# One more step of distance at four places of the second layer's interleaved chains, in a two-layer perceiver block on one core

## The chip, the core and the metric

The kernel runs on one core of one Trainium2 chip. The metric is the device time of one execution in microseconds (us), as the median of several runs. One execution was also recorded by the hardware profiler; times inside the kernel come from that record. The engines are TensorE (PE, with its weight loads shown as PEld), VectorE (DVE), ScalarE (ACT), GpSimd (POOL) and SyncE (SP, which issues most DMAs).

## The reference

Sixteen sequences of 64 tokens, 256 wide, pass through two layers. Each layer is cross-attention to a context of 1024 rows per sequence (16 heads of 16), then a self-attention, then a feed-forward part; before each part the rows are normalised, and the result is added to `x`.

```python
x = x + L0_xattn(layernorm(x), ctx_1024, ...)
x = x + L0_attn(layernorm(x), ...)
x = x + L0_ffn(layernorm(x), ...)       # top-2 of 8 experts
x = x + L1_xattn(layernorm(x), ctx_1024, bias, mask, ...)
x = x + L1_attn(layernorm(x), ...)      # rotary positions, softmax over 64
x = x + L1_ffn(layernorm(x), ...)       # silu(gate) * up, all operands quantised

# the second layer's feed-forward quantises x, h and the weights:
scale = max(abs(block of 16)) / 6
q = nearest of (0, .5, 1, 1.5, 2, 3, 4, 6) to abs(x / scale), with sign, times scale
```

All arithmetic is in 32-bit floats.

## The kernel before, in words

Only the second layer is touched. It starts in the profile at about 864 us and is one call of `cross_attention(1, ...)` that also carries the self-attention and the feed-forward part as side chains.

The 1024 rows of `x` are held as eight tiles `x[n]` of 128 rows, two sequences each. The cross-attention walks over 64 slots: 16 sequences, two halves of the heads (`dt`), two halves of the 1024 keys (`hf`). For each slot, PE makes four score products (`scores`, L567), sixteen transposes in four groups (`transpose_keys`, L597, four groups of four heads) and sixteen products with the values (`attend`, L611). DVE adds the mask to the scores and takes minima (L578), ACT takes the exponentials once both key halves are there (L589), and DVE and ACT copy the transposed weights out of PSUM (L226, L228). Key and value projections of sequences that were not made earlier stand in the slots too (`project`, L394 and L409); the first nine sequences have theirs loaded from DRAM, so from about 1130 us on each slot holds more PE work.

The side chains are Python generators. After each of the four groups of transposes of a slot, `advance()` lets every live chain go on to its next `yield`. A step is thus a quarter of a slot, and `bare(n)` is n steps in which the chain issues nothing. What a chain issues in a step stands on PE between two groups of transposes. Three kinds of chain are of interest:

- `outputs(b)` ends the attention of sequence b: ACT copies the sum `ot`, PE turns it (L633), DVE divides by the sums into `osb` (L636); after the second sequence of a pair, PE turns `osb` (L649), DVE adds a bias into `oT` (L653), and `project_rows` multiplies by the output weights (L322) and adds to `x[n]` (L324).
- `row_attention(n)` follows: normalisation on DVE (`layernorm_rows`, L258 to L275), turning (`transposed_rows`, L290 and L292), query and key products (L1373), rotation (L1393), value products (L1416), scores (L1428), softmax, the weights turned (L1452) and copied by ACT into `turned` (L228), their products with the values (L1468, L1479), the division (L1489, L1490) and the projection (L322).
- `feed_forward(n)` follows that: normalisation, `fp4` quantisation of the row (L1037 to L1053, ten DVE instructions in three steps), turning, gate and up products in two halves (`hidden`, L1520) with a silu on ACT (L1523), `fp4` of each half, `turn_hidden(0)` and `turn_hidden(3)` (L1530), and the down product (L1545).

A chain for tile n starts when its second sequence is done, every 32 steps (eight slots), and is longer than that, so the feed-forward part of tile n runs beside `outputs` and `row_attention` of tile n + 1. `queries(n)` is a further chain, not changed here. After the last slot, a loop advances the chains that are left two steps at a time, with nothing in between: there a bare step alone separates nothing.

PE's order is the program's (`tc.manual_schedule(engines={PE})`). The orders of DVE, ACT and POOL are made by the tile framework's scheduler when the program is built, from the program's order and its own estimates. All engines execute in order. PSUM has eight banks: one for the attention sums (`pso`), seven handed out in rotation to all other products (`bank()`, tiles `psw`): the eighth `bank()` after another waits until the tile of the first has been read.

Of the kernel before, what the change touches and what calls it, by code (L numbers as in the profile page):

```python
# [120 lines left out]
def kernel(ctx: ExitStack, tc: tile.TileContext, a: dict, out: bass.AP):  # L121
# [17 lines left out]
    def bank():  # L139
        return psum["w"].tile([P, 512], F32, name="psw")  # L140
# [18 lines left out]
    def colbias(name, dt):  # L159
        j = KC * COLB.index(name) + dt  # L160
        return colb[:, j : j + 1]
# [16 lines left out]
    def rowbias(name):  # L178
        j = ROWB.index(name)
        k = j - NB0 if j >= NB0 else j  # L180
        return rowb[j >= NB0][:, D * k : D * (k + 1)]
# [40 lines left out]
    def evacuate(dst, src, vector=None):  # L222

        turn[0] += 1
        if turn[0] % 2 if vector is None else vector:
            nc.vector.tensor_copy(dst, src)  # L226
        else:
            nc.scalar.copy(dst, src)  # L228
# [21 lines left out]
    def bare(n):  # L250

        for _ in range(n):
            yield
# [33 lines left out]
    def transposed_rows(pool, xn, name="xTr"):  # L287
        pt = bank()
        for c in range(KC):
            nc.tensor.transpose(pt[:, c * P : (c + 1) * P], xn[:, c * P : (c + 1) * P], ident)  # L290
        xT = pool.tile([P, KC, P], F32, name=name)
        nc.scalar.copy(xT, pt[:, : 2 * P].rearrange("p (c t) -> p c t", c=KC))  # L292
        return xT
# [24 lines left out]
    def project_rows(n, oT, w, bias=None):  # L318

        pm = bank()  # L320
        for c in range(KC):
            nc.tensor.matmul(pm[:, :D], oT[:, c, :], w[:, c, :], start=(c == 0), stop=(c == KC - 1))  # L322
        if bias is None:
            nc.vector.tensor_tensor(x[n], pm[:, :D], x[n], ALU.add)  # L324
            return
        t = small.tile([P, D], F32, name="prow")
        nc.vector.tensor_tensor(t, pm[:, :D], bias, ALU.add)
        nc.gpsimd.tensor_tensor(x[n], x[n], t, ALU.add)


    def cross_attention(layer, wq, wkv, wo, bq, bk, bv, bo, mask, keep, bias, after, ready, arrive, idle):
        side = "right" if layer else "left"
        with ExitStack() as st:
# [285 lines left out]
            def outputs(b):  # L619


                n, half = b // 2, b % 2
                ot = two.tile([P, KC, P], F32, name="ot")
                evacuate(ot, po.pop(b), False)
                yield
                yield
                rec = two.tile([P, NP], F32, name="rec")
                nc.vector.reciprocal(rec, sums[b])
                if half == 0:
                    osb[n] = two.tile([P, NP, 2, HD], F32, name="osb")  # L630
                pq = bank()
                for c in range(KC):
                    nc.tensor.transpose(pq[:, c * P : (c + 1) * P], ot[:, c, :], ident)  # L633
                pov = pq[:, :D].rearrange("p (r j d) -> p r j d", j=2, d=HD)
                for j in range(2):
                    nc.vector.tensor_tensor(  # L636
                        osb[n][half * SQ : (half + 1) * SQ, :, j, :],
                        pov[j * SQ : (j + 1) * SQ, :, j, :],
                        rec[j * SQ : (j + 1) * SQ, :].unsqueeze(2).to_broadcast([SQ, NP, HD]),
                        ALU.mult,  # L640
                    )
                if half == 0:
                    return
                yield
                yield
                pt = bank()
                rows = osb[n].rearrange("p r j d -> p (r j d)")
                for c in range(KC):
                    nc.tensor.transpose(pt[:, c * P : (c + 1) * P], rows[:, c * P : (c + 1) * P], ident)  # L649
                oT = two.tile([P, KC, P], F32, name="oT")  # L650
                for c in range(KC):

                    nc.vector.tensor_scalar(  # L653
                        oT[:, c, :], pt[:, c * P : (c + 1) * P], colbias(bv, c), None, ALU.add
                    )
                yield
                yield
                project_rows(n, oT, wo, None if layer else rowbias(bo))
# [361 lines left out]
    def fp4_tiles(pool, tag, most):  # L1020
        return (
            pool.tile([P, most], F32, name=f"t{tag}"),
            pool.tile([P, most], F32, name=f"m{tag}"),
            pool.tile([P, most // BLK], F32, name=f"scl{tag}"),
            pool.tile([P, most // BLK], F32, name=f"rsc{tag}"),
        )
# [323 lines left out]
    def last_layers(one):  # L1350
# [11 lines left out]
        def row_attention(n, two):  # L1362
# [2 lines left out]
            nc.gpsimd.tensor_tensor(x[n], x[n], rowbias("L1_attn_b_proj"), ALU.add)  # L1365
            yield from bare(4)
            xT = transposed_rows(two, xn)
            yield
            yield
            pm = bank()  # L1370
            for i, (w, dt) in enumerate((w, dt) for w in (wq, wk) for dt in range(KC)):
                for c in range(KC):
# [76 lines left out]
            for dt in range(KC):  # L1449
# [5 lines left out]
                        ident,  # L1455
                    )
                evacuate(eT[:, dt, :, :], pt.rearrange("p (g q) -> p g q", g=NG), False)
            yield
            yield


            po = [bank() for _ in range(2)]
# [38 lines left out]
        def feed_forward(n, two):  # L1501
            tok = slice(n * P, (n + 1) * P)
            alone = n == NT - 1
            xn = yield from layernorm_rows(two, n, "xnr", True)
            yield
            yield from fp4(fp4_tiles(one, "h", NI), xn, xn, P, D)
            yield from bare(2)
            xT = transposed_rows(two, xn)
            yield
            yield  # L1510
            h = one.tile([P, NI], F32, name="h")
            hT = one.tile([P, NCH, P], F32, name="hT")

            def hidden(cols):
                w = cols.stop - cols.start
                pg = bank()[:, :w]
                pu = bank()[:, :w]
                for ps, wt in ((pg, wgT), (pu, wuT)):
                    for c in range(KC):
                        nc.tensor.matmul(  # L1520
                            ps, xT[:, c, :], wt[:, c, cols], start=(c == 0), stop=(c == KC - 1)
                        )
                nc.scalar.activation(h[:, cols], pg, AF.Silu)  # L1523
                nc.vector.tensor_tensor(h[:, cols], pu, h[:, cols], ALU.mult)

            def turn_hidden(g):
                pt = bank()
                for j in range(3):
                    w = min(P, NI - (g + j) * P)
                    nc.tensor.transpose(  # L1530
                        pt[:w, j * P : (j + 1) * P], h[:, (g + j) * P : (g + j) * P + w], ident
                    )
                if g + 3 < NCH:
                    evacuate(hT[:, g : g + 3, :], pt[:, : 3 * P].rearrange("p (j t) -> p j t", j=3), False)
                else:
                    evacuate(hT[:, g : g + 2, :], pt[:, : 2 * P].rearrange("p (j t) -> p j t", j=2), False)
                    w = NI - (g + 2) * P
                    evacuate(hT[:w, g + 2, :], pt[:w, 2 * P : 3 * P], False)

            py = None  # L1540

            def down(g):
                for j in range(g, g + 3):
                    w = min(P, NI - j * P)
                    nc.tensor.matmul(py, hT[:w, j, :], wdT[:w, j, :], start=(j == 0), stop=(j == NCH - 1))  # L1545


            halves = [slice(0, 3 * P), slice(3 * P, NI)]
            if alone:

                hidden(halves[0])
                tiles = fp4_tiles(one, "h", NI)
                first = fp4(tiles, h[:, halves[0]], h[:, halves[0]], P, 3 * P)
                next(first)
                hidden(halves[1])
                for _ in first:
                    pass
                turn_hidden(0)
                py = bank()[:, :D]
                down(0)  # L1560
                for _ in fp4(tiles, h[:, halves[1]], h[:, halves[1]], P, NI - 3 * P, 3 * P):
                    pass
                turn_hidden(3)
                down(3)
            else:
                tiles = fp4_tiles(one, "h", NI)
                hidden(halves[0])
                yield
                yield from fp4(tiles, h[:, halves[0]], h[:, halves[0]], P, 3 * P)
                hidden(halves[1])  # L1570
                yield
                turn_hidden(0)
                yield
                yield from fp4(tiles, h[:, halves[1]], h[:, halves[1]], P, NI - 3 * P, 3 * P)
                yield from bare(2)
                turn_hidden(3)
                yield from bare(3)
                py = bank()[:, :D]
                down(0)
                down(3)  # L1580
            y = small.tile([P, D], F32, name="prow")
            nc.vector.tensor_tensor(y, py, x[n], ALU.add)
            nc.sync.dma_start(of[tok, :], y)
# [104 lines left out]
```

## Time and profile before

| | |
|---|---|
| device time, three runs | 1530.3, 1532.1, 1533.7 us (median 1532.1) |
| profiled execution: its own time, its span | 1533.16 us, 1531.1 us |
| mean granted PE clock | 0.949 of full speed |
| PE busy | 1393.2 us, 91% |
| DVE busy | 953.7 us, 62% |
| ACT busy | 759.2 us, 50% |
| POOL busy | 336.2 us, 22% |
| second layer: start, last slot, end | about 864, 1455 and 1528 us |

"Idle before" is the time that an engine stood still ahead of an instruction, and the releaser after the arrow is the instruction whose end let it go on. PE is the busy engine, and it executes in order, so a wait of PE in the slots delays everything behind it. The granted clock is the share of full clock that PE was given in a stretch; at 0.50 a product takes about twice as long.

### The profile page before, as it was taken

The page shows a single profiled execution, that of the slowest core. Times are in us where ns is not written, and L with a number is a line of the kernel's source. Part 1 is how long each engine was busy: PE and PEld are TensorE (multiplying, and loading weights), DVE is VectorE, ACT ScalarE, POOL GpSimd, SP SyncE. Part 2 cuts the span into 40 slices and gives each one's busy share as a digit, 9 for nine tenths or more (in the row PEclk, how much of TensorE's full clock was granted, in tenths as well). Part 3 has the DMA queues.
Part 4 walks back from the last instruction along what each step waited for, and adds up shares of the span by engine and source line. Part 5 has one row for each costly group of instructions (what it writes and reads, how often), then busy time and mean ns, then how long its engine had stood idle before and what let it go on. Part 6 is the DMA issues. An engine that isn't in the chain of part 4 may idle for free.

```text
span 1531.1 us, 33572 instructions
## 1 busy us (share of the span) xinstructions
PE 1393.2 (91%) x13796; PEld 997.1 (65%) x13796; DVE 953.7 (62%) x2573; ACT 759.2 (50%) x1385; POOL 336.2 (22%) x368
## 2 busy tenths in 40 slices
PE   6999999999999898999999789787889999999954
PEld 3677667776776655668888566565656767666732
DVE  3577767777777432365730277786867586767654
ACT  2565666565656531223221476665645555555620
POOL 4344443343332120013300022120201011110000
PEclk9999999999999999999999799898999999999977
DMA  6111101110101022277773332322101111000000
GB/s 231 59 36 40 52 32 33 37 58 33 32 29 56 37 96 71 92 262 230 253 277 120 125 125 98 128 80 77 52 22 35 49 53 49 22 26 1 5 1 7
DMA packets 53556, 119.53 MB, mean 78 GB/s; under 512 B 4908, under 2 KB 25004, under 8 KB 51100
## 3 DMA queue, kind: packets, MB, share of 16 engines
q1 hardware_dynamic: 50732, 112.21, 21.8%
q0 software_dynamic: 1568, 4.26, 1.0%
q8 instruction: 108, 1.77, 0.5%
q10 hardware_dynamic: 1104, 0.93, 0.2%
q14 instruction: 44, 0.36, 0.1%
HBM read 94.32 MB, written 23.07 MB: 77 GB/s over the span
## 4 chain that ended last, share of the span: by engine, by line
PE 72%; DVE 16%; ACT 6%; issue 3%; DMA 2%; POOL 1%; ACTq 0%; DVEq 0%; SPq 0%; POOLq 0%
PE psw L597 11%; PE psw L567 9%; PE pso L611 8%; PE psw L458 6%; PE psw L462 5%; DVE e L578 5%; ACT e L589 4%; PE psw L1227 4%; PE psw L796 4%; PE psw L1247 4%; PE psw L409 3%; PE psw L394 3%; PE psw L783 3%; PE psw L1520 2%; PE psw L1545 2%
## 5 line engine op out<-in xcount | busy, mean ns | idle before, releaser
L589 ACT ACTIVATE e<-e,mn 128x1024 f32<-128x1024 f32 x256 | 291.1, 1139 | 114.5 <-DVE mn L578 113.7
L597 PEld LDWEIGHTS psw<-consts,e 128*128 128x128 f32 x2048 | 240.5, 144 | 104.1 <-issue 62.4
L597 PE MATMUL psw<-consts,e 128*128 128x128 f32 x2048 | 287.3, 280 | 8.3 <-ACT e L589 4.3
L228 ACT COPY eT<-psw 128x512 f32<-128x512 f32 x384 | 209.3, 587 | 156.2 <-PE psw L597 156.2
L578 DVE CUSTOM_DVE_ANT_0 e<-psw,negb,mn 128x512 f32<-128x512 f32 x256 | 179.6, 747 | 138.6 <-PE psw L567 138.6
L578 DVE CUSTOM_DVE_ANT_0 e<-psw,negb 128x512 f32<-128x512 f32 x256 | 163.0, 685 | 67.4 <-PE psw L567 67.4
L567 PE MATMUL psw<-kT,qm 32*128 32x512 f32 x1024 | 170.4, 682 | 8.5 <-DVE mn L578 4.4
L611 PE MATMUL pso<-eT,v 128*32 128x128 f32 x4096 | 146.9, 287 | 0.0
L611 PEld LDWEIGHTS pso<-eT,v 128*32 128x32 f32 x4096 | 110.2, 114 | 27.7 <-issue 26.2
L226 DVE COPY eT<-psw 128x512 f32<-128x512 f32 x128 | 83.0, 682 | 7.5 <-PE psw L597 7.5
L567 PEld LDWEIGHTS psw<-kT,qm 32*128 32x128 f32 x1024 | 52.9, 195 | 42.5 <-issue 22.8
L796 PE MATMUL psw<-w_L_xattn_Wkv_w,actx 128*128 128x256 f32 x288 | 74.2, 411 | 2.2 <-issue 1.4
L359 POOL TENSOR_SCALAR negb<-m 128x1024 f32<-128x1024 uint8 x16 | 16.7, 1045 | 264.4 <-DVE mn L578 214.7
L783 PE MATMUL psw<-actx,w_L_xattn_Wkv_w 128*128 128x512 f32 x144 | 67.4, 608 | 1.3 <-DVE x L769 1.3
L796 PEld LDWEIGHTS psw<-w_L_xattn_Wkv_w,actx 128*128 128x128 f32 x288 | 58.4, 207 | 15.3 <-issue 5.0
L790 ACT ACTIVATE astage<-psw,colb 128x512 f32<-128x512 f32 x36 | 24.6, 687 | 80.8 <-PE psw L783 47.3
L462 PEld LDWEIGHTS psw<-wgT,actx 128*128 128x128 f32 x448 | 53.3, 192 | 10.6 <-ACT eT L228 5.3
L462 PE MATMUL psw<-wgT,actx 128*128 128x128 f32 x448 | 58.3, 278 | 0.0
L1227 PE MATMUL psw<-xeT,w 128*128 128x256 f32 x256 | 56.6, 380 | 0.8 <-issue 0.8
L1247 PE MATMUL psw<-w,hT 128*128 128x256 f32 x256 | 56.6, 379 | 0.0
L458 PE MATMUL psw<-actx,wgT 128*128 128x512 f32 x112 | 56.4, 605 | 0.0
L409 PE MATMUL psw<-w_L_xattn_Wkv_w,ctxT 128*128 128x256 f32 x224 | 55.6, 392 | 0.0
(282 smaller groups left out, 2255.9 us busy)
## 6 DMA issues: line engine op xcount, KB each, us to landing
ctxT<-in_ctxT_dram SPq DMA_DIRECT2D x23, 1024.0 KB, 5.0
w<-in_L_ffn_w_dram SPq DMA_DIRECT2D x16, 1024.0 KB, 6.5
actx<-in_ctxT_dram SPq DMA_DIRECT2D x9, 1024.0 KB, 5.5
kd<-astage SPq DMA_DIRECT2D x36, 256.0 KB, 4.0
vd<-astage SPq DMA_DIRECT2D x36, 256.0 KB, 2.5
kT<-kd SPq DMA_DIRECT2D x9, 1024.0 KB, 6.2
v<-vd SPq DMA_DIRECT2D x9, 1024.0 KB, 4.8
ab<-in_fside_BxS_dram SPq DMA_DIRECT2D x32, 256.0 KB, 3.5
```

Source lines behind the costliest of these rows:

```text
L228: nc.scalar.copy(dst, src)
L458: nc.tensor.matmul(pm, a_, x_, start=True, stop=True)
L462: nc.tensor.matmul(pm[:, cols], x_[:, cols], a_, start=True, stop=True)
L567: nc.tensor.matmul(sc[g], qm[b // 2][r : r + 32, dt, b % 2, :, :].rearrange("p j q -> p (j q)"), kT[b][r : r + 32, dt, cols], start=True, ...
L578: nc.vector.tensor_tensor_reduce(out=e[:, cols], in0=sc[g], in1=negb[b][:, cols], scale=1.0, scalar=3e38 if hf == 0 else mn[b][:, 0, pr : ...
L589: nc.scalar.activation(e, e, AF.Exp, scale=-1.0, bias=mn[b][:, 1, pr : pr + 1], accum_out=sums[b][:, pr : pr + 1])
L597: nc.tensor.transpose(pt[:, g * P : (g + 1) * P], es[b, dt, g][:, k * P : (k + 1) * P], ident)
L611: nc.tensor.matmul(po[b][32 * g : 32 * g + 32, dt, :], v[b][:, k, pr * 32 : (pr + 1) * 32], e[:, g, :], start=(k == 0), stop=(k == NK - 1),)
L783: nc.tensor.matmul(pm, w1kv[:, c, dt * P : (dt + 1) * P], actx[b][:, c, cols], start=(c == 0), stop=(c == KC - 1),)
L796: nc.tensor.matmul(pm[:, j * D : (j + 1) * D], actx[b][:, c, (k + j) * P : (k + j + 1) * P], w1kv[:, c, D : 2 * D], start=(c == 0), stop=( ...
L1227: nc.tensor.matmul(ph[:, j * CAP : (j + 1) * CAP], w1[:, c, (f + j) * P : (f + j + 1) * P], xeT[:, c, :], start=(c == 0), stop=(c == KC - 1),)
L1247: nc.tensor.matmul(py[:, j * D : (j + 1) * D], hT[:, f, j * P : (j + 1) * P], w2[:, f, :], start=(f == 0), stop=(f == FF // P - 1),)
```

## The change

Four waits of two bare steps become three: between `osb` and its turning (in the second layer alone), between the turning of the normalised row and the query and key products in `row_attention`, between the copies of the turned weights and the products with the values, and between the quantised second half of `h` and `turn_hidden(3)`. A chain is four steps, one slot, longer. Three of the places also lie on the way of the last chain, which is worked off after the last slot; the fourth does not, since `feed_forward(7)` takes another branch.

```diff
@@ outputs(b)
                 if half == 0:
                     return
-                yield
-                yield
+                yield from bare(3 if layer else 2)
                 pt = bank()
                 rows = osb[n].rearrange("p r j d -> p (r j d)")
@@ row_attention(n, two)
             yield from bare(4)
             xT = transposed_rows(two, xn)
-            yield
-            yield
+            yield from bare(3)
             pm = bank()
@@ row_attention(n, two)
                 evacuate(eT[:, dt, :, :], pt.rearrange("p (g q) -> p g q", g=NG), False)
-            yield
-            yield
+            yield from bare(3)

             po = [bank() for _ in range(2)]
@@ feed_forward(n, two)
                 yield from fp4(tiles, h[:, halves[1]], h[:, halves[1]], P, NI - 3 * P, 3 * P)
-                yield from bare(2)
+                yield from bare(3)
                 turn_hidden(3)
                 yield from bare(3)
```

No instruction of the computation is added or removed. The line numbers of what stands behind the edits move up by one to three.

## The prediction

> **What bounds the kernel now.** I read the page first: PE is busy 91% of the span and the chain that ended last lies on it for 72%. So I listed PE's groups by line, with the idle time before each, for the second layer alone (860 to 1460 us):
>
> ```profile
> L1373 PE MATMUL psw<-xTr,w_L_attn_w_qkv 128*128 128x128 f32 x112 | 15.6, 298 | 0.3
> L1468 PE MATMUL psw<-turned,vz 64*32 64x64 f32 x448 | 6.7, 236 | 11.4 <-ACT turned L228 10.9
> L1530 PE MATMUL psw<-consts,h 128*128 128x128 f32 (+1 forms) x36 | 6.1, 279 | 3.8 <-DVE mn L578 3.8
> L649 PE MATMUL psw<-consts,osb 128*128 128x128 f32 x16 | 4.3, 362 | 24.3 <-DVE osb L636 24.3
> ```
>
> The consumers of all four edits are here. Turning `osb` (L649) waits 24.3 us for DVE, the products with the turned weights (L1468) 10.9 us for ACT. The query and key products (L1373) wait 0.3 us, and L1530's 3.8 us stand before `turn_hidden(0)`; `turn_hidden(3)`, the fourth place, waits for nothing in the slots.
>
> PE's timeline gives the single waits. Before L649: 2.49, 4.53, 4.52, 3.61, 3.62, 3.61 and 1.95 us, one per pair of sequences. Before L1468: 3.64, 3.63 and 3.64, none once the slots hold key and value projections. One late `osb` wait:
>
> ```profile
> 1227.39 1.04 PE L597 MATMUL psw<-consts,e 128*128 128x128 f32 x8
> 1232.04 0.44 PE L649 MATMUL psw<-consts,osb 128*128 128x128 f32 x2 [3.62 <-DVE osb L636]
> 1232.41 1.42 PE L611 MATMUL pso<-eT,v 128*32 128x128 f32 x32
> 1233.76 2.09 PE L567 MATMUL psw<-kT,qm 32*128 32x512 f32 x8
> ```
>
> The columns are start, duration, engine, line and count. Behind the wait L567 takes 2.09 us instead of its usual 1.14. The windows show why a wait costs more than itself (PEclk is the third value from the end):
>
> ```profile
> 986.40:991.00 4.60, 0.07 (x2) 0.06 (x1) 4.47 (x13) 4.08 (x8) 3.38 (x3) 0.96 0.69 281
> 991.00:995.00 4.00, 4.00 (x42) 2.12 (x42) 2.51 (x9) 0.00 (x0) 0.15 (x1) 0.50 0.61 161
> 995.00:998.00 3.00, 3.00 (x16) 2.50 (x13) 2.35 (x8) 1.07 (x3) 0.00 (x0) 0.59 0.00 0
> 1440.00:1446.00 6.00, 6.00 (x35) 4.74 (x28) 1.61 (x6) 2.12 (x3) 0.00 (x0) 0.61 0.00 0
> ```
>
> In the 4.53 us wait PE did nothing while DVE was busy 4.47 of 4.60 us; then PE ran at half clock to about 996 us. DVE was late because the normalisation and row quantisation of tile n's feed-forward stood ahead of `osb` of tile n + 1.
>
> **What the edits move.** Times below are the profiled execution's (1533.2 us). Up to the first changed `osb` every engine's order is as before, and SP's is unchanged throughout. In the built order of the changed kernel, L649 stands behind one more L611, L567 and half the transposes of the next slot. The chain before is a slot longer, so the attention projection (L322) now stands in the same step as L633, and the normalisation it feeds falls behind `osb` on DVE, not ahead. The price: `oT` now stands behind that normalisation, the whole row quantisation and four minima; the output projection (L322) waits for it. That is what is late next.
>
> *Late pairs* (waits 3.61, 3.62, 3.61). I start a clock at L567, 1221.69 us. Before, the output projection ended at 1239.87, after 18.2 us. Moved ahead of it now: the attention projection 1.03, a value projection (L409) 1.9, four transposes 0.5, less a turning (L290) 0.2: 3.2 us of work. DVE in its new order: minima start 1.3 after L567, four at 0.68: 4.0; L402 and two L226: 5.8; L324 and `osb` 1.0: 6.8. PE comes to L649 at 12.8 or later: no wait. On DVE the normalisation, a reciprocal, an L402 and the block maximum follow, 4.4 us by their rows: 11.2; four minima with four short quantisation rows: 15.0; five more: 16.8; `oT`: 17.4. PE gets to the projection at 16.0, waits 1.6 and ends it at 18.6. Net 18.2 + 3.2 - 18.6 = 2.8; I take off 0.5, as short DVE rows stretch while POOL writes the mask (L1038 took 0.80 here instead of 0.17). Bounds per pair: 5.2 saved (wait plus 1.6 at half clock) to 3.4 lost (second rival). I take -2.3 three times: **-6.9**. For the pair at 1401, whose wait was 1.95 with no POOL work, the same sum gives about **0**.
>
> *Early pairs* (4.53, 4.52): the same count from 982.69. The output projection ended after 15.8; 1.25 is moved ahead; `osb` is ready at 6.4, `oT` at 14.2, PE at the projection by 9.5 to 10.5, so about 4 us of wait come back there, and it ends at 15.3. Net 1.7, twice: **-3.4**. Bounds: 7.1 saved to 3 lost.
>
> *First pair* (2.49): no feed-forward runs yet, nothing takes its place: **-2.5**.
>
> *Turned weights.* ACT copied `turned` behind four exponentials of 1.13 (968.5 to 973.05), PE waited from 970.0 to 973.67. One more step puts L611, L567 and eight transposes between. The exponentials still stand ahead, and the fourth score bank and the next transposes wait for ACT copies: I count PE through L1479 10.5 us after L567, eight transposes (0.9) ahead; before it needed 12.4 to do the rest. Net 2.8, three times: **-8.4**. Bounds per pair: 4.8 (wait and slower rows behind it) to 1.
>
> *Query and key products, `turn_hidden(3)`:* no wait to remove; they shift what follows. The row scores L1428 waited 1.86 and 1.85 us for ACT's `qm` (its bank); now they find score banks that DVE frees about 1.4 us late in three early pairs: **0**, bounds -4 to +4. On POOL `rqm` (0.94) falls behind the three mask instructions (1.04 + 2.49), ready about 8.7 after L567, PE there at 9.0: hidden, 0.3 us of cover in the first pairs.
>
> *ACT table loads.* Both silus now fall between two groups of exponentials: 34 loads become 22.
>
> ```profile
> L1523 ACT ACT_TABLE_LOAD x14 | 18.0, 1283 | 0.2
> L589 ACT ACT_TABLE_LOAD x13 | 16.7, 1283 | 0.2
> ```
>
> 12 x 1.283 = 15.4 us of ACT, mostly beside PE work: **-1**, bounds 0 and -8.
>
> *The end.* After the last slot nothing covers. L1468 and L1479 of tile 6 (1.4 us) now stand behind the last L611. Their division on DVE (1.77 + 0.42) is cut by `osb`, so L324 of x[6] starts 6.1 after L611's end, not 1.8; the way on to the turning (L290) gets 0.65 shorter, as `oT` is then done. L290 comes 3.6 later, less 1.3 of work gone from the slots: **+2.3**, bounds +1 to +4.
>
> Sum: -6.9 - 3.4 - 2.5 - 8.4 - 1 + 2.3 = -19.9, so 1513.3 in place of 1533.2. The median of the runs is 1.1 below the profiled execution: **1512 us**.
>
> [...] After the 1.95 us wait at 1401 the clock stayed at 1.00; after 1.90 at 1014, L1373 ran 3.56 us instead of 1.95. The rows therefore leave open whether the waits that I leave (1.3 to 4 us) cost up to 1.6 each. [...]
>
> **Rivals.**
> 1. *Nothing takes the waits' place:* 35.2 us (24.3 + 10.9) go, and with them half clock of 2.6 twice, 1.6 three times, 1.2 three times (13.6): -48.8 + 2.3, 1487 as profiled, 1486 as median. Against it: DVE is busy 28.9 of 32 us from 982 to 1014. Chance 0.10 for anything below 1497.
> 2. *Slower: `oT` becomes the wait.* If DVE serves `oT` more than 5 us after PE has arrived at the output projection (the old wait plus its half clock), six pairs lose: 6 + 2.6 against 5.2, +3.4 each, 20.4; with -8.4, -2.5 and +2.3, 11.8 slower: 1544. For it: ten quantisation rows and 2.7 us of minima really stand ahead. Against: in the late pairs 3.2 us more PE work covers it. Chance 0.13.
> 3. *`osb` only changes its name:* the output projection waits as long as L649 did; -8.4 - 2.5 + 2.3 = -8.6: 1523.5. Chance 0.15.
> 4. *The clock eats it:* short bank waits follow each other and hold the clock down. At 1436 us, with waits of no more than 0.17, it was 0.72 for 4 us and 0.61 for 6: 3.5 us lost. Six pairs of that are 21: 1533, no change. [...] Chance 0.07.
>
> That the edit does not do what it says is ruled out by the built order.
>
> **How the numbers follow.** Forecast (1498 to 1521) 0.55; rivals 0.10, 0.13, 0.15, 0.07. A measurement tells about 0.2%, 3.1 us, from no change. Faster: 0.55 + 0.10 + 0.15 = 0.80; same 0.07; slower 0.13. Range 1497 to 1534: it leaves out the first rival's lower half and the second.
>
> **What would show it.** L649 without a wait in the second layer; L322 on `oT` with 1 to 2 us in late pairs and about 4 in early ones; L1468 below 1.5 per early pair; table loads 12 fewer; L290 after the last slot 2 to 4 us later behind L611. Waits over 5 us before L322, or PEclk of the layer no higher, would prove the forecast wrong.

## The result

The changed kernel takes 1516.2 us (median of four runs, 1513.8 to 1521.5), the kernel before 1532.9 (1530.3 to 1534.8): a ratio of 0.990 with a 95% interval of 0.986 to 0.993, faster by some 1%. The forecast was 1512. The profiled execution of the changed kernel was the slowest of its four (1521.49 us, span 1519.5, mean clock 0.955), so where its trace is set against the trace of before (1533.16), 11.7 us are to be explained, not the 16.7 of the medians. One single execution of all the experiments, of the first dose of the longer `osb` wait, was in a slow state (1985.7 us at a mean clock of 0.646, where the other three took 1517.6 to 1518.3) and counts in no ratio.

### The profile page after: what moved, and what is told of

It is laid out like the page before. It is cut to its first block, busy times and chain, and to the rows that moved or that the text cites. A ratio compares the mean times of both kernels' runs of the same rounds, so it can differ in the third digit from the quotient of the medians.

```text
span 1519.5 us, 33552 instructions
## 1 busy us (share of the span) xinstructions
PE 1391.2 (92%) x13796; PEld 994.4 (65%) x13796; DVE 961.1 (63%) x2573; ACT 744.7 (49%) x1373; POOL 338.5 (22%) x368
## 4 chain that ended last, share of the span: by engine, by line
PE 70%; DVE 16%; issue 5%; ACT 5%; DMA 3%; POOL 1%; ACTq 0%; DVEq 0%; POOLq 0%; SPq 0%
PE psw L597 10%; PE psw L567 8%; PE pso L611 7%; PE psw L458 6%; DVE e L578 5%; PE psw L462 5%; PE psw L795 4%; PE psw L1226 4%; PE psw L1246 4%; ACT e L589 4%; PE psw L394 3%; PE psw L782 3%; PE psw L1517 3%; PE psw L409 2%; PE psw L1542 2%
## 5 line engine op out<-in xcount | busy, mean ns | idle before, releaser
L589 ACT ACTIVATE e<-e,mn 128x1024 f32<-128x1024 f32 x256 | 291.1, 1139 | 119.1 <-DVE mn L578 119.1
L567 PE MATMUL psw<-kT,qm 32*128 32x512 f32 x1024 | 171.9, 659 | 11.1 <-ACT qm L537 6.6
L611 PE MATMUL pso<-eT,v 128*32 128x128 f32 x4096 | 140.9, 280 | 0.0
L611 PEld LDWEIGHTS pso<-eT,v 128*32 128x32 f32 x4096 | 106.2, 111 | 22.3 <-issue 21.9
L567 PEld LDWEIGHTS psw<-kT,qm 32*128 32x128 f32 x1024 | 53.5, 190 | 48.8 <-issue 20.1
L359 POOL TENSOR_SCALAR negb<-m 128x1024 f32<-128x1024 uint8 x16 | 16.7, 1045 | 253.1 <-DVE mn L578 202.8
L462 PEld LDWEIGHTS psw<-wgT,actx 128*128 128x128 f32 x448 | 53.3, 192 | 10.6 <-issue 5.3
L1233 ACT ACTIVATE hT<-psw 128x512 f32<-128x512 f32 x32 | 19.0, 597 | 75.4 <-PE psw L1226 75.4
```

Source lines behind the costliest of these rows:

```text
L462: nc.tensor.matmul(pm[:, cols], x_[:, cols], a_, start=True, stop=True)
L567: nc.tensor.matmul(sc[g], qm[b // 2][r : r + 32, dt, b % 2, :, :].rearrange("p j q -> p (j q)"), kT[b][r : r + 32, dt, cols], start=True, ...
L589: nc.scalar.activation(e, e, AF.Exp, scale=-1.0, bias=mn[b][:, 1, pr : pr + 1], accum_out=sums[b][:, pr : pr + 1])
L611: nc.tensor.matmul(po[b][32 * g : 32 * g + 32, dt, :], v[b][:, k, pr * 32 : (pr + 1) * 32], e[:, g, :], start=(k == 0), stop=(k == NK - 1),)
```

## The profile after

PE's groups in the second layer (860 to 1460 us), the columns as before: busy time, mean ns of one, idle time before and its releaser.

```profile
L1517 PE MATMUL psw<-wgT,xTr 128*128 128x384 f32 (+1 forms) x52 | 21.8, 548 | 11.5 <-ACT xTr L292 11.5
...
L1371 PE MATMUL psw<-xTr,w_L_attn_w_qkv 128*128 128x128 f32 x112 | 15.3, 296 | 0.0
L322 PE MATMUL psw<-w_L_xattn_out_w,oT 128*128 128x256 f32 x32 | 10.6, 462 | 12.0 <-DVE oT L652 12.0
...
L1527 PE MATMUL psw<-consts,h 128*128 128x128 f32 (+1 forms) x36 | 6.2, 285 | 0.0
...
L1465 PE MATMUL psw<-turned,vz 64*32 64x64 f32 x448 | 6.0, 224 | 0.0
...
L648 PE MATMUL psw<-consts,osb 128*128 128x128 f32 x16 | 3.2, 285 | 1.9 <-DVE osb L636 1.7
```

The two waits of before are gone: 24.3 us ahead of the turning of `osb` (now L648) are 1.9, of which 1.7 behind the last slot, and 11.4 ahead of the products with `turned` (now L1465) are 0.0. In their place stand 12.0 ahead of the output projection (L322, on `oT`) and 11.5 ahead of the gate products (L1517, on `xTr`). The first of these the forecast had, the second not.

One late pair on PE's timeline (start, duration, engine, line, count):

```profile
1225.94 0.38 PE L648 MATMUL psw<-consts,osb 128*128 128x128 f32 x2
1226.16 0.60 PE L597 MATMUL psw<-consts,e 128*128 128x128 f32 x4
1226.59 1.92 PE L409 MATMUL psw<-w_L_xattn_Wkv_w,ctxT 128*128 128x256 f32 x8
1228.35 0.60 PE L597 MATMUL psw<-consts,e 128*128 128x128 f32 x4
1230.56 1.13 PE L322 MATMUL psw<-w_L_xattn_out_w,oT 128*128 128x256 f32 x4 [1.61 <-DVE oT L652]
```

`osb` is turned without a wait, and the wait for `oT` is 1.61, 1.61, 1.62 and 1.61 in the four late pairs; the forecast's sum had 1.6. The L322 behind it is at full pace, and the windows show the clock and, at the end, what does not go so well (PEclk is the third value from the end of a line):

```profile
1226.00:1232.00 6.00, 4.38 (x27) 3.63 (x25) 4.86 (x17) 2.44 (x5) 0.00 (x0) 1.00 0.01 1
...
1443.00:1446.75 3.75, 3.53 (x8) 2.53 (x8) 1.18 (x4) 0.00 (x0) 0.00 (x0) 0.54 0.00 0
```

The new wait in the early pairs, on the timeline of all engines (PE and ACT lines from one answer):

```profile
1007.50 1.15 ACT L589 ACTIVATE e<-e,mn 128x1024 f32<-128x1024 f32 x1 [3.68 <-DVE mn L578]
...
1010.91 1.13 ACT L589 ACTIVATE e<-e,mn 128x1024 f32<-128x1024 f32 x1
...
1011.95 0.19 ACT L589 ACTIVATION_READ_ACCUMULATOR e<-e,mn 128x1 f32 x1
1012.04 0.35 ACT L292 COPY xTr<-psw 128x256 f32<-128x256 f32 x1
...
1012.45 1.11 PE L1517 MATMUL psw<-wgT,xTr 128*128 128x384 f32 x2 [4.09 <-ACT xTr L292]
```

PE waits 4.09 us until ACT has done four exponentials and then the copy of the quantised row; ACT itself could start them only when DVE had the minima, after standing still for 3.68 us. Before, four exponentials stood in the same way ahead of the copy into `turned`, four slots earlier. The large waits on `xTr` are two, in stretches 3 and 4 of the table below, where `turned` had three, in stretches 2 to 4.

The table loads on ACT, second layer:

```profile
L1520 ACT ACT_TABLE_LOAD x8 | 10.3, 1283 | 0.1
...
L589 ACT ACT_TABLE_LOAD x7 | 9.0, 1283 | 0.1
...
L1444 ACT ACT_TABLE_LOAD x1 | 1.3, 1283 | 0.0
```

27 have become 15 at the two lines that load in turn (L1523 and L589 before), twelve fewer, as forecast.

Where the time went, by stretches of eight slots. The marks are ends of `attend` (L611), which the change doesn't move against the slots, eight slots apart; the first lies 27.1 us into the layer before and 27.5 after, and the rest goes up to the last L611. The row "the same program again" is from the trace of the experiment with a shorter end, below, whose program differs from the changed one only behind stretch 7; DVE, ACT and POOL execute the same instructions in the same order up to there.

| stretch | 1 | 2 | 3 | 4 | 5 | 6 | 7 | rest |
|---|---|---|---|---|---|---|---|---|
| before, us | 47.9 | 64.2 | 73.6 | 84.1 | 85.5 | 85.5 | 82.2 | 40.7 |
| after, us | 45.1 | 67.5 | 72.1 | 74.0 | 82.1 | 82.1 | 82.1 | 40.2 |
| the same program again, us | 45.1 | 63.9 | 68.6 | 73.8 | 82.1 | 82.1 | 82.1 | (40.2) |
| forecast of the difference | -2.5 | -4.5 | -4.5 | -5.1 | -2.3 | -2.3 | 0 | 0 |
| after less before | -2.8 | +3.3 | -1.5 | -10.1 | -3.4 | -3.4 | -0.1 | -0.5 |
| again less before | -2.8 | -0.3 | -5.0 | -10.3 | -3.4 | -3.4 | -0.1 | |
| PE at half clock, us: before | 6.8 | 10.2 | 13.7 | 17.1 | 3.4 | 3.4 | 0 | 6.8 |
| after | 0 | 22.7 | 17.5 | 4.2 | 0 | 0 | 0 | 0 |
| the same program again | 0 | 16.3 | 10.6 | 3.8 | 0 | 0 | 0 | 0 |

The forecast row is the prediction's own terms (first pair, early pairs, turned weights, late pairs) put at the stretch in which the old wait stood. Up to the last L611 after is 18.1 shorter from the layer's start, where the prediction had 21.2 and 1 for the table loads. The layer starts 1.0 later in this execution, though nothing was changed ahead of it, and what follows the last L611 is 5.4 longer (73.1 to 78.5): 18.1 - 1.0 - 5.4 = 11.7.

## Experiments

Two theories were set against each other. Theory 1: an edit is worth the waits that it covers. Theory 2: the edits shift the chains' work on VectorE and ScalarE against the slots, and any of them can move any wait; what they bring depends on what stands ahead of what, and on whether a wait throws PE to half clock. A third, that the twelve table loads made ACT free earlier, had a run of its own. All were timed in three rounds; ratios are to the kernel before on the same chip, so they, not the medians, compare runs of different groups.

**Attention rows alone.**

```diff
-                yield
-                yield
+                yield from bare(3 if layer else 2)
                 pt = bank()
```

> Only the first edit: three bare steps between osb and its turning, in the second layer. Theory 1 (each edit covers its own wait): L649's 24.3 us of waits fall below 4 us; the normalisation stays ahead of osb on DVE here, so oT is not pushed behind it and the output projection waits under 1 us; 10 to 18 us faster than before. Theory 2 (the gain comes from all edits together making the chain a whole slot longer): the wait returns at the output projection, under 6 us faster.

Measured: 1517.4 us, ratio 0.9911 (0.9894 to 0.9928), 12.8 us faster, as Theory 1 had it. PE's groups in the second layer:

```profile
L322 PE MATMUL psw<-w_L_xattn_out_w,oT 128*128 128x256 f32 x32 | 10.4, 453 | 1.5 <-DVE oT L652 1.5
...
L1467 PE MATMUL psw<-turned,vz 64*32 64x64 f32 x448 | 6.9, 255 | 9.4 <-ACT turned L228 9.4
L290 PE MATMUL psw<-consts,xnr 128*128 128x128 f32 x30 | 6.7, 319 | 13.4 <-DVE xnr L1052 12.3 <-DVE xnr L275 1.1
...
L648 PE MATMUL psw<-consts,osb 128*128 128x128 f32 x16 | 3.2, 285 | 0.7 <-DVE osb L636 0.6
```

The `osb` wait goes, and only 1.5 comes back on `oT`: alone, this edit has little of the forecast's price. In the early pairs part of it turns up ahead of L290, on the quantised row (2.39 and 2.85 us). A late stretch takes 82.6, of which only 0.6 are waits that the trace shows; 1 us more than with the products alone is in the score products (L567: 22.7 against 20.6 us in two such stretches, though one takes 641 ns in both). Why those take longer stays open.

**Turned weights alone** (the third edit of the diff).

> Only the third edit: three bare steps between the copies of the turned weights and their products. Theory 1: L1468's 10.9 us of waits fall below 4 us, L649 keeps about 24 us, 5 to 9 us faster. Theory 2: the wait for ACT moves to another product (score banks, ot), L649 changes by more than 5 us although its distance is as before; within 4 us of before.

Measured: 1518.9 us, ratio 0.9917 (0.9899 to 0.9934). PE's groups:

```profile
L1467 PE MATMUL psw<-turned,vz 64*32 64x64 f32 x448 | 6.9, 249 | 9.5 <-ACT turned L228 9.4
...
L649 PE MATMUL psw<-consts,osb 128*128 128x128 f32 x16 | 4.0, 337 | 20.8 <-DVE osb L636 20.8
```

The edit does not take away the wait that it stands at: 9.5 of 11.4 are left (3.14 in place of 3.64 each), because the four exponentials stay ahead of the copy. It gains by another wait: the late `osb` waits fall from 3.62 to 2.44. Both theories miss: 11.3 us were gained, where Theory 1 had 5 to 9 and Theory 2 at most 4.

**Self-attention products alone** (the second edit).

> Only the second edit: three bare steps between the turned row and the query and key products, which waited 0.3 us. Theory 1: nothing to remove, within 3 us of before. Theory 2 (position): table loads fall from 34 to 22 in the built order as in the whole change, 15.4 us of ACT; 3 to 8 us faster by shorter ACT waits (qm, turned).

Measured: 1510.5 us, ratio 0.9867 (0.9851 to 0.9884). PE's groups:

```profile
L322 PE MATMUL psw<-w_L_xattn_out_w,oT 128*128 128x256 f32 x32 | 8.3, 383 | 0.5 <-DVE oT L653 0.5
...
L1467 PE MATMUL psw<-turned,vz 64*32 64x64 f32 x448 | 7.0, 259 | 9.4 <-ACT turned L228 9.4
...
L649 PE MATMUL psw<-consts,osb 128*128 128x128 f32 x16 | 3.9, 332 | 20.8 <-DVE osb L636 20.8
```

An edit at a place that had 0.3 us of wait brings 19.6 us, as much as all four (the intervals overlap); Theory 1 had at most 3 and Theory 2 3 to 8, so both miss, though the way is Theory 2's. Up to the last L611 it has the changed kernel's time (573.0 us from the layer's start, 572.6 there), and the end keeps its length: 71.6 us against 78.5. Theory 1 can't be held as it stands. The two runs before and this one share what Theory 2 names: a chain one step longer ahead of the feed-forward part, a late stretch of 82.4 to 82.6 in place of 85.5, and at most one spell at half clock from 1150 to 1400 us (the stretch with it took 84.2). What the shift does shows on DVE in a late pair. Before, three rows of the row quantisation (L1039, L1041 and L1042, 1.87 us) stood ahead of the first half of `osb`:

```profile
1230.61 0.41 DVE L1042 TENSOR_TENSOR th<-xnr,rsch 128x256 f32<-128x256 f32 x1
1231.05 0.28 DVE L636 TENSOR_TENSOR osb<-psw,rec 64x128 f32<-64x128 f32 x1
```

With the products a step later they stand behind it, and the wait is 2.44 in place of 3.62:

```profile
1218.15 0.28 DVE L636 TENSOR_TENSOR osb<-psw,rec 64x128 f32<-64x128 f32 x1
1218.46 0.25 DVE L1039 RECIPROCAL rsch<-sclh 128x16 f32<-128x16 f32 x1
```

**Turned feed-forward values alone** (the fourth edit).

> Only the fourth edit: three bare steps before turn_hidden(3), which waits for nothing in the slots. Table loads stay 34. Both theories: within 2 us of before; a rival (the whole change's loss in the early pairs comes from the longer feed-forward) would have it 3 us or more slower.

Measured: 1530.0 us, ratio 0.9996 (0.9981 to 1.0011): no change, table loads still 34. It stands behind what the others shift.

**No silu table.** In the kernel before, the gate's silu is replaced by a copy, so silu is left out of the computation and ACT loads 7 tables instead of 34.

```diff
-nc.scalar.activation(h[:, cols], pg, AF.Silu)
+nc.scalar.activation(h[:, cols], pg, AF.Identity)
```

> The kernel before, every distance as it was, with the silu of the gate left out (ACT copies the gate product in its place), so that ACT has 7 table loads instead of 34. Theory 3 (much of the gain comes from the table loads that a shift by a step saves): late waits before L649 fall from 3.61 to 2 to 2.8 us, the granted clock from 1150 us on is 1.00, 10 to 18 us faster than before. Theory 1 (distances): waits as before within 0.5 us, under 5 us faster.

Measured: 1525.2 us, ratio 0.9964 (0.9949 to 0.9978). The waits in the slots stay (L649 24.3 us, `turned` 3.64 each); of the 5 us gained 4.3 are behind the last L611 (68.8 us in place of 73.1), where nothing covers ACT. So 27 loads fewer bring next to nothing in the slots, and the theory of the table loads falls; the prediction's -1 for twelve was about right.

**Gate products one step later as well** (the changed kernel, and a third step between `xTr` and the gate products).

```diff
             xT = transposed_rows(two, xn)
-            yield
-            yield
+            yield from bare(3)
             h = one.tile
```

> The whole change, and three bare steps in place of two between the turning of the feed-forward's row and its gate and up products, which wait 11.5 us for ACT in the changed kernel (4.09 in two early pairs, 0.7 in late ones). Theory A (what the change loses in the early pairs is this wait): the wait falls below 3 us and the kernel is 5 to 10 us faster than the whole change. Theory B (DVE and ACT are the limit of the early pairs, a wait removed comes back elsewhere): within 3 us of the whole change.

Measured: 1510.3 us, ratio 0.9864 (0.9841 to 0.9886). The wait on `xTr` fell only from 11.5 to 8.2, not below 3: as with `turned` alone, a step more does not get past the four exponentials. Whether it gains on the changed kernel (0.9897, 0.9864 to 0.993) these runs don't settle.

**`oT` on ScalarE** (the changed kernel, the bias of `oT` added by ACT in the second layer).

```diff
+                    if layer:
+                        nc.scalar.activation(
+                            oT[:, c, :], pt[:, c * P : (c + 1) * P], AF.Identity, bias=colbias(bv, c)
+                        )
+                        continue
                     nc.vector.tensor_scalar(
```

> The whole change, with the bias added into oT by ACT instead of DVE in the second layer. Theory 1 (L322 waits because oT stands behind the row quantisation in DVE's order): its 12.0 us of waits fall below 3 us, late pairs go from 82.1 us to about 80.5, 5 to 12 us faster than the whole change. Rival (the wait only moves to ACT's exponentials or to the score banks): L322 or its neighbours keep over 8 us, within 3 us of the whole change.

Measured: 1500.5 us, ratio 0.9807 (0.9787 to 0.9826), the fastest of all. PE's groups:

```profile
L1521 PE MATMUL psw<-wgT,xTr 128*128 128x384 f32 (+1 forms) x56 | 23.9, 556 | 13.1 <-ACT xTr L292 13.1
...
L322 PE MATMUL psw<-w_L_xattn_out_w,oT 128*128 128x256 f32 x32 | 10.0, 441 | 0.2
```

The 12.0 us ahead of L322 are gone, stretches 5 to 7 take 80.5 each in place of 82.1, and `xTr` takes back 1.6. So `oT` behind the normalisation and the row quantisation on DVE, the price that the prediction named, is what the change pays. The rest of the gain lies in the early stretches, where half clock plays in: stretch 2 takes 57.4 us here with 3.4 at half clock.

**A shorter end** (the changed kernel, with two steps again at the turned weights of the last two tiles).

```diff
-            yield from bare(3)
+            yield from bare(3 if n < NT - 2 else 2)
```

> The whole change, but with two bare steps again ahead of the turned weights' products of the last two tiles alone. The time from the last L611 to the end falls from 78.5 us to 72 to 75 us and the kernel is 2 to 5 us faster than the whole change; if the longer end came from the clock or from osb instead, it stays above 77 us and the time is the same.

Measured: 1512.7 us, ratio 0.9888 (0.9858 to 0.9919). The end stays at 78.3, but the edit does not reach what it was meant to undo: the products with tile 6's turned weights still start as the last L611 ends (1426.33 us, 1437.43 in the changed kernel), whereas before, and in the four kernels with one of the edits, they start 3.2 to 3.9 us earlier. So the run doesn't test the prediction's reason for the longer end. It is worth more for what it shows by the way. Up to stretch 7 its program is the changed kernel's, its large waits are the same to 0.02 us, and yet stretches 2 and 3 took 63.9 and 68.6 in place of 67.5 and 72.1. Windows of the two executions around the same place of the program, first the changed kernel:

```profile
1033.00:1036.50 3.50, 2.42 (x40) 1.52 (x38) 3.47 (x4) 3.50 (x10) 3.23 (x3) 1.00 0.48 175
1036.75:1047.25 10.50, 10.19 (x82) 7.55 (x85) 6.51 (x20) 4.16 (x10) 0.89 (x2) 0.51 0.21 52
```

and this run:

```profile
1025.30:1028.80 3.50, 2.42 (x40) 1.53 (x38) 3.47 (x4) 3.50 (x9) 3.29 (x3) 1.00 0.43 177
1029.10:1039.60 10.50, 10.18 (x115) 7.39 (x115) 9.17 (x29) 6.57 (x13) 0.91 (x2) 1.00 0.16 51
```

PE was busy 2.42 of 3.50 us in both, with the same wait of 1.08 us. In one execution some 10.2 us at half clock followed, in the other none. The half-clock time is thus partly chance, and a single trace's early stretches carry some 7 us of it: stretches 2 to 4 took 213.5 us in the changed kernel's trace and 206.3 in this one.

**`oT` on ScalarE alone** (on the kernel before).

> The kernel before with one edit: in the second layer the bias that makes oT is added on ScalarE instead of VectorE; no distance is changed. In before no L322 waits for oT by more than about half a microsecond in all. Theory 1 (each edit is worth the waits that it covers): nothing to cover, 1528 to 1532. Theory 2 (what counts is where the chain's VectorE work falls, and whether the osb wait of a late pair, 3.62 us in before, ends below about 2.5 us so that the clock stays at 1.00): 16 tiles' worth of short biases (5.5 us in the second layer, 346 ns each) leave VectorE, but they stand behind osb in the queue, not ahead of it, so the osb wait stays near 3.6, the late pair near 85.5 and the time at 1525 to 1531.

Measured: 1527.8 us, ratio 0.9983 (0.9966 to 1.0000). Late `osb` waits 3.61 and 3.62 as before: at most a small gain. Theory 2 had that, Theory 1 is 0.2 off; the same edit is worth 1% only where the change has made `oT` late.

**Products and `oT` on ScalarE** (the second edit of the diff, and `oT`'s bias on ACT).

> Two edits on the kernel before: the self-attention products one bare step later (the edit that alone gave 1510.5) and oT's bias on ScalarE in the second layer. Attention rows, turned weights and turned feed-forward values keep their distances of before. Theory 1: the waits on osb (20.8 us with the products alone) and on turned (9.4) are still there, no oT wait was there to take away (0.5), so 1508 to 1512, and the 1500.5 of the whole change with the same bias is out of reach. Theory 2: the shorter VectorE chain brings the late osb waits from 2.44 down by about the length of one or two biases (0.3 to 0.7 each), late pair 81 to 82, 1502 to 1509.

Measured: 1514.9 us, ratio 0.9899 (0.9876 to 0.9923). Theory 2's number fails: the late `osb` waits stay at 2.44 and 2.45, those on `osb` and `turned` at 20.8 and 9.4 in all, as Theory 1 said, though the time is some 3 us above its range as well. The trace shows why it is not below the products alone. One late wait in this run:

```profile
1220.19 0.69 PE L649 MATMUL psw<-consts,osb 128*128 128x128 f32 x2 [2.45 <-DVE osb L636]
1220.80 1.94 PE L611 MATMUL pso<-eT,v 128*32 128x128 f32 x32
1222.67 2.09 PE L567 MATMUL psw<-kT,qm 32*128 32x512 f32 x8
```

and the same place with the products alone:

```profile
1219.10 0.44 PE L649 MATMUL psw<-consts,osb 128*128 128x128 f32 x2 [2.44 <-DVE osb L636]
1219.47 1.08 PE L611 MATMUL pso<-eT,v 128*32 128x128 f32 x32
1220.48 1.14 PE L567 MATMUL psw<-kT,qm 32*128 32x512 f32 x8
```

The waits are equal; in the first the clock fell for 6.8 us (from 1219.75 to about 1226.6) and the stretch took 85.4 instead of 82.4. A wait of 2.4 us was met by half clock in one case and not in the other.

**A longer `osb` wait, two doses.** The kernel with the products alone, with the multiplications into the second half of `osb` done twice, then three times, in late tiles.

```diff
-                for j in range(2):
+                for j in range(2) if not (layer and half and n >= 4) else [0, 1] * 2:
```

> The kernel with the products' edit alone (1510.5, late osb waits 2.44 to 2.45 us, late pair 82.4, clock 1.00 there), with the two VectorE multiplications that write the second half of osb done twice in the second layer's tiles from n = 4 on (two more of 64x128, 288 ns each, the same values): the osb wait of each late pair grows by about 0.58 to 3.0 us. Theory 2 with a clock that falls only behind a wait of between 2.5 and 3.6 us: if that limit is above 3.0, late pair 83.0, clock 1.00, 1512 to 1515; if it is below, late pair 85 or more. Without any limit (waits cost their own length): late pair 83.0, 1512 to 1515 too; the next run tells these apart.

> As the run before it, with the two multiplications done three times (four more of 288 ns): the osb wait of each late pair grows by about 1.15 to 3.6 us, as long as in the kernel before. Theory 2 with the clock limit: after a wait of 3.6 the clock is halved for the next stretch, the late pair goes to 85 to 86 and the granted clock of the late stretch to 0.96 to 0.98, as in the kernel before; 1520 to 1527. Without a limit: late pair 83.5 to 83.6, clock 1.00, 1514 to 1517.

Measured: 1518.0 us, ratio 0.9926 (0.9902 to 0.9950), and 1524.1, ratio 0.9967 (0.9954 to 0.9980), against 0.9867 without a dose. The first dose made the waits longer than meant: 3.75, 3.75 and 2.91 (2.44, 2.45 and 1.60 without), since other DVE instructions (L1041 and L1042) were ordered in between; so it did not stop at 3.0, and its time is above the range of both theories. The second gave 4.38, 4.37 and 3.53. The wait of the last late pair in the first dose:

```profile
1386.40:1389.30 2.90, 0.00 (x0) 0.00 (x0) 2.65 (x10) 0.88 (x2) 0.00 (x0) 1.00 0.00 0
1389.30:1393.00 3.70, 3.69 (x48) 2.44 (x49) 3.49 (x12) 0.00 (x0) 0.00 (x0) 1.00 0.00 0
```

and in the second:

```profile
1387.30:1390.80 3.50, 0.02 (x1) 0.00 (x0) 3.23 (x11) 0.90 (x2) 0.00 (x0) 1.00 0.00 0
1391.00:1394.50 3.50, 3.50 (x42) 1.95 (x41) 2.29 (x8) 0.00 (x0) 0.00 (x0) 0.51 0.00 0
```

Behind the wait of 2.91 us the clock stayed at 1.00, behind that of 3.53 it was half for 3.4 us. Stretch 5 with its wait of 3.75 or 4.38 takes 85.3 and 85.9, against 82.4 with 2.44: 2.9 more for 1.3 of wait, 3.5 more for 1.9. In both 1.6 is left over, about what half clock over 3.4 us costs if a product takes twice as long there (1.7, an estimate). The second run's 1524.1 lies in the range of the theory with a limit (1520 to 1527), above that without one (1514 to 1517).

Taken over the nine traces of this case that have late `osb` waits, from 1130 to 1420 us: all 17 waits of 3.53 to 4.38 us were met by a stretch at half clock, 3 of 11 waits of 2.44 or 2.45, neither the one of 2.91 nor the seven of 1.59 to 1.95. In the changed kernel, whose late waits are 1.6, none was.

## Why the prediction was right, and where it was not

The sign, the size and the main path were right: 16.7 us by the medians for a forecast of 20, the time in the range, the waits on `osb` and `turned` gone, `oT` late in their place, and its bias the thing to move next. That the total came so near is in part luck: in the profiled execution stretches 2 and 3 fell short of their terms by 10.8 us and the end by 3.1, while stretches 4 to 6 gave 7.2 more than theirs. Point by point:

- *Late pairs.* Forecast -2.3 each and 0 for the pair at 1401; the two full stretches give -3.4 and -3.4, the one with the wait at 1401 -0.1. The wait on `oT` came out at 1.61 where the sum had 1.6. The 0.5 taken off for stretched DVE rows was not needed: the short scale row (L1038 before, L1037 after) took 378 ns on average before and takes 174 after. The first late pair's wait (1145 us) lies in stretch 4, which gained 10.1 for 5.1 forecast; there PE spent 17.1 us at half clock before and 4.2 after. The late waits were right and the forecast per pair 1.1 too small; the half clock that went in stretch 4 was in no term.
- *First pair.* -2.5 forecast, -2.8 measured.
- *Early pairs and turned weights.* -4.5 for each of stretches 2 and 3 was forecast; +3.3 and -1.5 came in the profiled execution, -0.3 and -5.0 in the other of the same program. This is the step that failed. `oT` waits 2.23 there, not about 4; but other waits that the sum did not have came in. "The exponentials still stand ahead" was followed for `turned` and not for what else ACT serves from the same queue: in the longer chain the copy of `xTr` falls behind four of them, and 4.09 us come back at L1517 in stretch 3 and again in stretch 4. In stretch 2 the two old waits (8.2 us) went, and with `oT` came a wait for the query rows of the unchanged chain `queries`, on DVE:

```profile
949.25 0.66 PE L290 MATMUL psw<-consts,xnq 128*128 128x128 f32 x2 [2.33 <-DVE xnq L275]
```

  With 1.06 on the normalised row and smaller ones, all waits of stretch 2 are 8.6 us after 9.5, those of stretch 3 9.1 after 12.6. What is left of the loss is half clock: 12.5 us more of it in stretch 2 and 3.8 more in stretch 3 of the profiled execution, 6.1 more and 3.1 less in the other. No term had it. That the gain of this term was not the turned edit's is shown by the run with it alone, where the wait stays at 9.5. A reading was off too: the half clock behind the wait at 991 lasts to about 997.5 by the prediction's own windows (0.50 over 4 us, 0.59 over 3), not to 996, so the 2.6 us that the first rival took for it are some 3.2.
- *Table loads.* Twelve fewer, and worth next to nothing in the slots (the run without silu).
- *Query and key products, `turn_hidden(3)`.* At 0 the term misses what the second edit does alone: 20 us, by shifting the chain. What it adds beside the others no run shows. The fourth is 0 alone.
- *The end.* +2.3 forecast, +5.4 in the trace. The turning (L290) of tile 6's feed-forward comes 17.2 us after the last L611, 11.0 before: 6.2 later for 3.6 forecast. The prediction counted the division cut by `osb`; it missed that the two projections (L322) then fall in a half-clock stretch (2.05 and 1.76 us, 1.13 in the late pair above at a clock of 1.00), so L324 of `x[6]` starts 7.8 us after the last L611, not 6.1. And the way from there to the turning is not 0.65 shorter but 9.4 us, where it was 9.1; DVE works off two normalisations by turns there, before as well:

```profile
1443.22 2.05 PE L322 MATMUL psw<-w_L_attn_w_proj,oT 128*128 128x256 f32 x4 [1.16 <-DVE oT L1487]
1445.06 1.76 PE L322 MATMUL psw<-w_L_xattn_out_w,oT 128*128 128x256 f32 x4
1451.37 0.66 PE L290 MATMUL psw<-consts,xnr 128*128 128x128 f32 x2 [4.56 <-DVE sclh L1037]
1454.71 0.66 PE L290 MATMUL psw<-consts,xnr 128*128 128x128 f32 x2 [2.67 <-DVE xnr L1052]
```

  The runs with one edit have ends of 70.8 to 71.6; those with all four, where tile 6's products with the turned weights fall behind the last L611, 75.2 to 78.5. Which two edits make it long was not tried.

*The rivals.* "Nothing takes the waits' place" is refuted by L322 and L1517. "`oT` becomes the wait" is right in kind and wrong in size: 1.6 and 2.2 us, where more than 5 would have decided. "Only changes its name" is true in part of `turned` and `xTr` (three waits of 3.64, two of 4.09), not of `osb`. "The clock eats it" is false for the late pairs (clock 1.00 throughout) and bears on the early ones, where PE was at half clock for 22.7 us of stretch 2 though no wait in it was above 2.33 us; what held the clock there is not shown.

*What the waits left cost.* The prediction left open whether waits of 1.3 to 4 us cost up to 1.6 us each beyond their length; its sum counted none of that. In the late pairs the wait of 2.91 us was met by no half clock, and those of 3.53 to 4.38 us all were; in the traces of before and of the two doses the half-clock stretches around them last 3.4 or 6.8 us. Waits of 2.44 or 2.45 us were met by half clock 3 times in 11, and the stretch with PE busy 2.42 of 3.50 us was followed by it in one execution and not in the other, with the same program up to there. The prediction's two rows, 1.90 us at 1014 with half clock behind it and 1.95 at 1401 without, are one more such pair. What decides it is not shown.

What is open: the 2 us of the late stretch with attention rows alone, what the second edit adds beside the other three, the split of the longer end, and whether `oT` on ScalarE in a kernel with a short end goes below 1500.5, which was not tried.

## What to carry to other kernels

A wait at the end of a queue that several chains share does not belong to the place where it is seen: more steps can move it to whatever comes to stand behind the same kind of instructions (here from `turned` to `xTr`), so list all that the delaying engine serves in that stretch, not only the consumer that is being moved. Don't price a PE wait by its length alone: here no late wait of 1.6 us was met by half clock, all 17 of 3.53 us and more were, for some 1.6 us more in the two stretches compared, and of those of 2.44 or 2.45 us 3 in 11 were. Put each edit on the chip alone before adding them up: here 14, 13, 20 and 1 us, by the ratios, made 16 together.

## What the runs showed of the hardware

Two executions with the same program and the same waits differ by some 10.2 us of half clock at one place, and by 7.2 us of time over three stretches with 13.6 us of half clock between them. From 860 to 1460 us the half-clock spells in the traces of before and after lasted about 3.4, 6.8 or 10.2 us, one of them 20.5. One spell of the changed kernel went on for some 10.2 us while PE was busy (10.19 of 10.50 us at a granted clock of 0.51).
